# Two PSUM evictions on VectorE moved from the end of one unit behind two additions in the next

## The chip, the cores and the metric

The kernel runs on one core of one Trainium2 chip. The metric is the device time of one execution in microseconds (us); each figure for a kernel is the median over its runs. Everything is fp32.

## The reference, cut to what matters

There are 64 graphs of 256 nodes with 256 features each, and one adjacency matrix `adj` (256 x 256, sparse, symmetric pattern) for all of them. Four layers follow each other: three message-passing layers (L0, L1, L3) and one attention layer (L2).

```python
def gnn(h_t, A_a, A_m, W1, b1, W2, b2, Wa, ba, Wm, bm, beta1, beta2, beta3):
    pre_u = einsum('bud,dk->buk', h_t, W1[:d])
    pre_v = einsum('bvd,dk->bvk', h_t, W1[d:])
    hidden = relu(pre_u[:, :, None, :] + pre_v[:, None, :, :] + b1)
    S = sigmoid(einsum('buvk,ko->buvo', hidden, W2)[..., 0] + b2[0])
    a_t = einsum('buv,bud->bvd', S * A_a, h_t)
    m_t = einsum('uv,bud->bvd', A_m, h_t) * h_t
    return beta1*h_t + beta2*(a_t @ Wa + ba) + beta3*(m_t @ Wm + bm)

def attention(data, W1, W2, b2, bias2):          # bias1 is adj
    feats = einsum('bni,oi->bno', data, W1)
    f1 = einsum('bno,o->bn', feats, W2) + b2[0]
    coefs = softmax(leaky_relu(f1[:, :, None] + f1[:, None, :]) + adj, -1)
    return einsum('bij,bjo->bio', coefs, feats) + bias2 + data
```

`S * A_a` is needed only where `adj` is not zero, so scores are worked out for edges alone. The change concerns `m_t`.

## The kernel before, in words

Graphs go through in pairs (g = 0, 1), and the pairs in two streams, `a` and `b`, of 16 pairs each. A unit of work sets the scores of one stream's pair (the heavy part, `scores`) beside the light part of the other stream's pair; then the streams change places. With 32 pairs and three message-passing layers there are 96 such units. `beside` draws steps from both generators, but what runs when is set by the framework, which orders each engine's instructions when the program is built. The order is then fixed, and each engine goes through its own queue.

The light part of a unit, in order:

- `spread` (L787, L789): two halves, m = 0 and 1. TensorE multiplies the weighted edges `rm` with the one-hot matrix `gu` into a PSUM tile, 16 matmuls for each half, and VectorE adds each tile to `sa`, the score matrix (two additions of 128x512).
- `finish`: two products `sa` x `h` (L281, eight matmuls of 128x256 each), copied by ScalarE to `aT` (L344); then the products with Wm (of `mT`) and Wa (of `aT`), L366 or in the last layer L352, added to the kept part `hb` by VectorE.
- in layer L1 only, `attention` (L401 to L451).
- `before`: the products with W1 (L625), from which ScalarE makes `pu` (L626) and VectorE `pv` (L627) and `own` (L636); SyncE stores `pu` and `pv` to tables in DRAM (L630).
- `mixed`, at the very end: for each graph the product of `adj` and `h` (L281, eight matmuls, one PSUM tile), which VectorE multiplies with `hT` into `mT` (L316). These two multiplications are what the change moves. `mT` is read one unit later than the next one, when the same stream is the light part again.

The heavy part rates edges. Some come as `ga` tiles, made by TensorE in PSUM from `pre` and the one-hot `pick` (L697, two matmuls for a tile), some as `fetched` rows, which GpSimd gathers from the tables by indirect DMA (L742), some from `own`. VectorE turns each half tile into scores with one instruction (L661, into `junk` with an accumulator `raw`). When the scores of a half are complete, ScalarE makes `val` from `raw` (L681 and L682), and VectorE `rm` from `val` in four instructions (L689). `early` makes the first part of `sa` (L771 on TensorE, L775 on VectorE). The second half's `val` and `rm` close the unit: they come in `end()`, after `mixed`, and `spread` of the next unit needs them:

```python
            made, got, end = scores(*heavy)
            for step in light:
                ...
            for tiles in (got, made):
                for _ in tiles:
                    pass
            end()
```

PSUM has two pools: `ps`, five tiles, for all products, and `ga`, three tiles. `mT`, `hT` are single tiles for each stream.

The boundary between two units is the stretch from the products of `mixed` to `finish` of the next unit. Boundaries repeat in six kinds. They are numbered from the start: boundary n is of kind n modulo 6, and the first eight matmuls of boundary 0 start at 25.5 us of the span. What follows a boundary:

| kind | light part of the unit that follows | its length, us (usual) |
|---|---|---|
| 1 and 2 | finish L0, before L1 | 32.1 and 33.3 to 36 |
| 3 and 4 | finish L1, attention, before L3 | 43.6 and 42.8 |
| 5 and 0 | finish L3, store, before L0 of the next pair | 30.9 and 31.3 |

Boundaries used as examples below: kind 2 at 1206 us, kind 3 at 1242, kind 4 at 1286, kind 5 at 1329, kind 0 at 1360, kind 1 at 1391.

Of the kernel before, what the change touches and what calls it, by code (L numbers as in the profile page):

```python
# [9 lines left out]
FP = mybir.dt.float32  # L10
I32 = mybir.dt.int32
AF = mybir.ActivationFunctionType
ALU = mybir.AluOpType
AX = mybir.AxisListType

P = 128
B, N, D = 64, 256, 256
# [36 lines left out]
def blk(c):  # L54
    return slice(c * P, (c + 1) * P)


def quarter(q):
    return slice(q * 64, (q + 1) * 64)
# [19 lines left out]
def adj_seq_kernel(ctx: ExitStack, tc: tile.TileContext, a: dict, out: bass.AP):  # L79
# [14 lines left out]
    nc = tc.nc  # L94
# [171 lines left out]
    def stages(pools):  # L266
        fm, wk, one, ps, ga = (pools[k] for k in ("fm", "wk", "one", "ps", "ga"))
# [6 lines left out]
        def psum():  # L274
            return ps.tile([P, 2, 256], FP, tag="ps", name="ps")

        def product(o, lhs, rhs):

            for m in range(2):
                for c in range(2):  # L280
                    mm(out=o[:, m, :], lhsT=lhs[:, c, blk(m)], rhs=rhs[:, c, :], start=c == 0, stop=c == 1)  # L281
# [25 lines left out]
                nc.sync.dma_start(out=h, in_=of_graph(a["x"], st["b"] + g))  # L307
                st["h"].append(h)

        def mixed(st, l):  # L310

            mT = one.tile([P, 2, 2, N], FP, tag="mT" + st["side"], name="mT")
            for g in range(2):
                t = psum()
                product(t, st["h"][g], adj)
                nc.vector.tensor_tensor(mT[:, :, g, :], t, st["hT"][:, :, g, :], ALU.mult)  # L316
                yield 0
            st["mT"] = mT

        def kept(st, l):  # L320

# [71 lines left out]
        def attention(st):  # L393
# [44 lines left out]
            for g in range(2):  # L438
# [16 lines left out]
                st["h"].append(h)  # L455

        return dict(psum=psum, product=product, load=load, mixed=mixed, finish=finish, attention=attention)

    def few(stack):
        pools = open_pools(stack)
        wk, one, ga = pools["wk"], pools["one"], pools["ga"]
        s = stages(pools)
        psum, mixed, finish, attention, load = (s[k] for k in ("psum", "mixed", "finish", "attention", "load"))
# [133 lines left out]
        def before(st, l):  # L599

            hT = st["hT"]
            pu = one.tile([P, 2, 2, D], FP, tag="pu" + st["side"], name="pu")
            pv = one.tile([P, 2, 2, D], FP, tag="pv" + st["side"], name="pv")
            pre = one.tile([P, len(FAST), 2 * D], FP, tag="pre" + st["side"], name="pre")
            flat = lambda t: t.rearrange("p m g d -> p m (g d)")
            order = [(m, g) for m in range(2) for g in range(2)]
            if l == LAST:
                order = [(m, g) for g in range(2) for m in range(2)]

            got = {LAST: (1, 0, 1, 1), GNN[1]: (1, 1, 1, 1), GNN[0]: (0, 0, 2, 1)}[l]  # L610
            got = dict(zip(order, got))
            st["tables"] = [
                tables.tile([N, 2 * D], FP, tag="table" + t + st["side"], name="table" + t) for t in "uv"
            ]

            own = one.tile([P, 2, 2, D], FP, tag="own", name="own")
            st["pu"], st["pv"], st["pre"], st["own"] = pu, pv, pre, own
            t = one.tile([P, FIRST, 2, D], FP, tag="fetched" + st["side"], name="fetched")
            st["fetched"] = [t[:, f] for f in range(FIRST)]
            for m, g in order:  # L620
                if l == LAST and (m, g) == (1, 0):
                    st["flip"](1)
                t = psum()
                for c in range(2):
                    mm(out=t, lhsT=hT[:, c, g, blk(m)], rhs=w1[l][:, c], start=c == 0, stop=c == 1)  # L625
                nc.scalar.copy(pu[:, m, g, :], t[:, 0, :])  # L626
                nc.vector.tensor_tensor(pv[:, m, g, :], t[:, 1, :], b1row[l], ALU.add)  # L627
                if g == 1:
                    for rows, x in zip(st["tables"], (pu, pv)):
                        nc.sync.dma_start(out=rows[blk(m)], in_=flat(x)[:, m])  # L630
                    if m == 0:
                        st["fetches"] = list(FETCHES)

                        if numbered:
                            fetch(st, AHEAD)
                nc.vector.tensor_tensor(own[:, m, g, :], t[:, 0, :], pv[:, m, g, :], ALU.add)  # L636
                if g == 1:
                    if m == 0:
                        rows_u(st, 0, 2, 0, 0)
                    rows_v(st, 2 - 2 * m, 2, 0)  # L640
                yield 0, got[(m, g)]
                if l == GNN[1] and (m, g) == (0, 1):
                    st["turn"](0)
                    yield 1
                    st["turn"](1)
                    yield 0, 1
            yield REST_OF_IT
            yield from mixed(st, l)

        def scores(st, l):  # L650

# [77 lines left out]
        def fetch(st, n):  # L729

            now, st["fetches"] = st["fetches"][:n], st["fetches"][n:]
            for f, x in now:
                rows = st["tables"][x]
                if f < 0:
                    to, ids = st["left"], (left_u, left_v)[x]
                    rows = rows.rearrange("n (g d) -> (n g) d", g=2)
                else:
                    to, ids = st["fetched"][f].rearrange("p g d -> p (g d)"), (ids_u, ids_v)[x][:, f : f + 1]
                    if f < FIRST:
                        rows = rows[blk(0)]  # L740
                with tc.issue_after(fetches[-1]) if fetches else nullcontext():
                    this = nc.gpsimd.indirect_dma_start(  # L742
                        out=to, out_offset=None, in_=rows, in_offset=bass.IndirectOffsetOnAxis(ap=ids, axis=0),
                        compute_op=(ALU.bypass, ALU.add)[x],
                    )
                fetches.append(this.ins)

        def rows_u(st, f, n, k, m):

            h = halves[k]  # L750
            nc.scalar.copy(  # L751
                st["pre"][h, f : f + n],
                st["pu"][h, m].rearrange("p g d -> p (g d)").unsqueeze(1).to_broadcast([64, n, 2 * D]),
            )

        def rows_v(st, f, n, k):

            for n in range(f, f + n):
                i = FAST[n][2]
                nc.scalar.copy(  # L760
                    st["pre"][halves[1 - k], n], st["pv"][halves[i % 2], i // 2].rearrange("p g d -> p (g d)")
                )
# [17 lines left out]
        def spread(st, l):  # L780

            rm, sa = st["rm"], st["sa"]
            for m in range(2):
                t = psum()
                for i in range(4):
                    for k, h in enumerate(halves):
                        mm(out=t[h, :, quarter(i)], lhsT=gu[:, k, 4 * m + i, :], rhs=rm[:, k, 4 * m + i],  # L787
                           start=True, stop=True)
                nc.vector.tensor_tensor(sa[:, m], sa[:, m], t, ALU.add)  # L789
            yield 1 if l == GNN[1] else 2  # L790

        def after(st, l):
            yield 1
            yield from spread(st, l)
            yield from finish(st, l)

        def stream(side, starts):

            sts = [{"b": b, "side": side} for b in starts]
            load(sts[0])  # L800
            short = [before(sts[0], GNN[0])]
            for i, st in enumerate(sts):
                yield short, (st, GNN[0])
                yield [after(st, GNN[0]), before(st, GNN[1])], (st, GNN[1])
                yield [after(st, GNN[1]), attention(st), before(st, GNN[2])], (st, GNN[2])
                short = [after(st, GNN[2])]
                if i + 1 < len(sts):
                    load(sts[i + 1])
                    short = [halfway(after(st, GNN[2]), 4, before(sts[i + 1], GNN[0]), 2)]
            yield short, None  # L810
# [26 lines left out]
                    pass  # L837
            end()

        past, numbered, fetches = [], [], []  # L840
        one_, two = stream("a", range(0, B, 4)), stream("b", range(2, B, 4))
        a_, b_ = next(one_), next(two)
        for _ in steps(a_[0]):
# [81 lines left out]
    with branch.Else():  # L925
        with ExitStack() as stack:
            few(stack)
# [32 lines left out]
```

## Time and profile before

| what | us |
|---|---|
| median of 3 runs (3524.08 to 3527.32) | 3524.88 |
| the profiled execution, its own time | 3531.84 |
| the profiled execution, its span | 3529.9 |
| TensorE matmul busy | 3446.7 |
| VectorE busy | 2605.4 |
| GpSimd busy | 2227.1 |
| ScalarE busy | 1599.5 |

The mean granted TensorE clock was 0.992. In the profile's lines PE is TensorE's matmuls, PEld its weight loads, DVE VectorE, ACT ScalarE, POOL GpSimd and SP SyncE. L316 is line 316 of the kernel. A group's line gives: line, engine, operation, written tile <- read tiles, shapes, count | busy us, mean ns of one | idle us of the engine just before them <- what ended that idle time. A line of the timeline gives: start us, length us, engine, line, operation, tiles, count [idle before <- what ended it]. A line of the chain gives: start us, length us, what. Start times are from the start of the span.

### The profile page before, as it was taken

The numbers are of one execution on the slowest core, as the hardware profiler recorded it, in microseconds if no ns is written. First come the engines' busy times: TensorE is split into PE (matmuls) and PEld (weight loads), VectorE is DVE, ScalarE is ACT, GpSimd is POOL, SyncE is SP. The second block draws the span as 40 slices with busy tenths as digits, with TensorE's granted clock in tenths as the row PEclk, the third lists the DMA queues.
The fourth block names the chain that finished last, engine by engine and source line by source line (L and its number), as shares of the span: only waits on it lengthen the run. The fifth ranks groups of instructions, "written<-read, shape, count | busy, mean of one in ns | idle before, by whom it ended". The sixth has DMA issues, their size and how long they took to land.

```text
span 3529.9 us, 48385 instructions
## 1 busy us (share of the span) xinstructions
PE 3446.7 (98%) x14328; PEld 2106.0 (60%) x14328; DVE 2605.4 (74%) x10584; ACT 1599.5 (45%) x2929; POOL 2227.1 (63%) x1754
## 2 busy tenths in 40 slices
PE   6999999999999999999999999999999999999998
PEld 3566565656656566565666656556565665656655
DVE  5777686777867777777777777768677787777776
ACT  2444444444444444444545445444444444444452
POOL 3747667576665757667576675766757566675754
PEclk7999999999999999999999999999999999999999
DMA  5768777687777867778687776867768677786865
GB/s 148 163 141 192 155 178 168 160 182 155 182 157 170 176 146 188 150 181 181 145 191 161 178 172 151 188 153 185 163 162 179 150 187 157 176 177 146 192 150 114
DMA packets 274733, 587.25 MB, mean 166 GB/s; under 512 B 37024, under 2 KB 54304, under 8 KB 274464
## 3 DMA queue, kind: packets, MB, share of 16 engines
q0 software_dynamic: 190464, 427.93, 60.7%
q1 hardware_dynamic: 82416, 154.96, 12.7%
q8 instruction: 116, 1.90, 0.2%
q10 hardware_dynamic: 1584, 1.20, 0.1%
q14 instruction: 153, 1.25, 0.1%
HBM read 466.51 MB, written 117.44 MB: 165 GB/s over the span
## 4 chain that ended last, share of the span: by engine, by line
PE 72%; DVE 11%; DMA 5%; POOL 5%; issue 5%; ACT 2%; ACTq 0%; POOLq 0%; DVEq 0%
PE ga L697 14%; PE ps L281 13%; PE ps L625 13%; PE ps L366 10%; PE ps L352 5%; POOL fetched L742 4%; PE ps L787 4%; PE ps L448 3%; DVE junk L661 3%; PE ps L407 3%; DMA fetched<-tablev,ids_v 3%; DVE rm L689 3%; PE ps L287 2%; DVE sa L775 2%; PE ps L401 2%
## 5 line engine op out<-in xcount | busy, mean ns | idle before, releaser
L742 POOL DMA_INDIRECT fetched<-tablev,ids_v x768 | 1210.7, 1576 | 355.3 <-issue 232.6
L742 POOL DMA_INDIRECT fetched<-tableu,ids_u x768 | 764.8, 996 | 824.1 <-DMA tableu<-pu 594.0
L697 PE MATMUL ga<-pre,pick 128*128 128x512 f32 x1536 | 769.7, 605 | 11.7 <-DVE junk L661 8.4
L625 PE MATMUL ps<-L_gnn_w,hT 128*128 128x512 f32 x1536 | 695.5, 596 | 5.8 <-DMA hT<-in_xT_dram 5.8
L661 DVE SCALAR_TENSOR_TENSOR junk<-ga,L_gnn_w2row 128x256 f32<-128x256 f32 x1536 | 582.7, 418 | 134.6 <-PE ga L697 122.6
L661 DVE SCALAR_TENSOR_TENSOR junk<-fetched,L_gnn_w2row 128x256 f32<-128x256 f32 x1536 | 595.1, 417 | 35.1 <-DMA fetched<-tablev,ids_v 35.0
L760 ACT COPY pre<-pv 64x512 f32<-64x512 f32 x768 | 473.5, 616 | 108.8 <-DVE pv L627 86.7
L625 PEld LDWEIGHTS ps<-L_gnn_w,hT 128*128 128x128 f32 x1536 | 285.1, 191 | 334.7 <-issue 313.6
L751 ACT COPY pre<-pu 64x1024 f32<-64x1024 f32 x384 | 392.9, 1039 | 3.9
L369 DVE TENSOR_TENSOR hT<-hb,ps 128x512 f32<-128x512 f32 x128 | 88.0, 687 | 412.9 <-PE ps L366 412.9
L697 PEld LDWEIGHTS ga<-pre,pick 128*128 128x128 f32 x1536 | 274.7, 191 | 179.2 <-issue 122.4
L281 PE MATMUL ps<-adj,h 128*128 128x256 f32 x1536 | 358.7, 386 | 11.1 <-DVE own L636 8.0
L281 PE MATMUL ps<-sa,h 128*128 128x256 f32 x1536 | 362.4, 385 | 3.7 <-issue 2.9
L281 PEld LDWEIGHTS ps<-sa,h 128*128 128x128 f32 x1536 | 290.3, 192 | 109.0 <-issue 46.2
L626 ACT COPY pu<-ps 128x256 f32<-128x256 f32 x384 | 142.4, 371 | 466.9 <-PE ps L625 443.2
L281 PEld LDWEIGHTS ps<-adj,h 128*128 128x128 f32 x1536 | 283.4, 190 | 80.0 <-issue 36.8
L330 ACT ACTIVATE hb<-hT,L_gnn_zbias,scas 128x512 f32<-128x512 f32 x128 | 97.4, 807 | 450.3 <-DVE hT L369 356.7
L689 DVE TENSOR_TENSOR rm<-gva,val 128x256 f32<-128x256 f32 x768 | 279.0, 417 | 9.7 <-ACT val L682 7.2
L787 PEld LDWEIGHTS ps<-rm,gu 128*64 128x64 f32 x3072 | 172.4, 137 | 139.2 <-PE ps L281 55.4
L787 PE MATMUL ps<-rm,gu 128*64 128x128 f32 x3072 | 215.9, 280 | 30.9 <-DVE rm L689 29.4
L344 ACT COPY aT<-ps 128x512 f32<-128x512 f32 x192 | 112.6, 586 | 293.2 <-PE ps L281 250.3
L366 PE MATMUL ps<-mT,L_gnn_Wm 128*128 128x512 f32 x512 | 240.6, 592 | 0.0
(155 smaller groups left out, 4200.2 us busy)
## 6 DMA issues: line engine op xcount, KB each, us to landing
tableu<-pu SPq DMA_DIRECT2D x192, 256.0 KB
tablev<-pv SPq DMA_DIRECT2D x192, 256.0 KB
hT<-in_xT_dram SPq DMA_DIRECT2D x32, 512.0 KB
h<-in_x_dram SPq DMA_DIRECT2D x64, 256.0 KB
out_dram<-h SPq DMA_DIRECT2D x64, 256.0 KB
fetched<-tableu,ids_u POOLq DMA_INDIRECT x768
fetched<-tablev,ids_v POOLq DMA_INDIRECT x768
L_gnn_w<-in_L_gnn_W_dram SPq DMA_DIRECT2D x6, 256.0 KB
```

The lines of the kernel that those rows point to most:

```text
L281: mm(out=o[:, m, :], lhsT=lhs[:, c, blk(m)], rhs=rhs[:, c, :], start=c == 0, stop=c == 1)
L352: mm(out=z[:, m, :], lhsT=y[:, c, g, blk(m)], rhs=w[:, c, :], start=j == 0 and c == 0, stop=j == 1 and c == 1)
L366: mm(out=z, lhsT=w[:, c, blk(m)], rhs=y[:, c], start=j == 0 and c == 0, stop=j == 1 and c == 1)
L625: mm(out=t, lhsT=hT[:, c, g, blk(m)], rhs=w1[l][:, c], start=c == 0, stop=c == 1)
L626: nc.scalar.copy(pu[:, m, g, :], t[:, 0, :])
L661: nc.vector.scalar_tensor_tensor(junk, t, 0.0, w2row[l], ALU.max, ALU.mult, accum_out=raw[:, i : i + 1])
L689: nc.vector.tensor_tensor(rm[:, k, ms, g, :], gva[:, k, ms, :], val[:, i : i + 4].unsqueeze(2).to_broadcast([P, 4, 64]), ALU.mult)
L697: mm(out=t, lhsT=pick[:, k, 4 * m + i, :], rhs=pre[:, n], start=True, stop=True)
L742: this = nc.gpsimd.indirect_dma_start(out=to, out_offset=None, in_=rows, in_offset=bass.IndirectOffsetOnAxis(ap=ids, axis=0), compute_op=( ...
L751: nc.scalar.copy(st["pre"][h, f : f + n], st["pu"][h, m].rearrange("p g d -> p (g d)").unsqueeze(1).to_broadcast([64, n, 2 * D]),)
L760: nc.scalar.copy(st["pre"][halves[1 - k], n], st["pv"][halves[i % 2], i // 2].rearrange("p g d -> p (g d)"))
L787: mm(out=t[h, :, quarter(i)], lhsT=gu[:, k, 4 * m + i, :], rhs=rm[:, k, 4 * m + i], start=True, stop=True)
```

## The change

`mixed` can now put its two multiplications on a list, `later`, in place of issuing them. `before` passes that list from the third unit's boundary on (where `past`, the list of ended score halves, isn't empty). `spread` of the next unit takes them from the list after its second addition, and issues them with an order-only dependence on that addition (`issue_after`). The two PSUM tiles of `mixed` are so held until then.

```diff
-        def mixed(st, l):
+        def mixed(st, l, later=None):
 
-            mT = one.tile([P, 2, 2, N], FP, tag="mT" + st["side"], name="mT")
+            st["mT"] = mT = one.tile([P, 2, 2, N], FP, tag="mT" + st["side"], name="mT")
             for g in range(2):
                 t = psum()
                 product(t, st["h"][g], adj)
-                nc.vector.tensor_tensor(mT[:, :, g, :], t, st["hT"][:, :, g, :], ALU.mult)
+                times = (mT[:, :, g, :], t, st["hT"][:, :, g, :], ALU.mult)
+                if later is None:
+                    nc.vector.tensor_tensor(*times)
+                else:
+                    later.append(times)
                 yield 0
-            st["mT"] = mT
...
             yield REST_OF_IT
-            yield from mixed(st, l)
+            yield from mixed(st, l, later if past else None)
...
         def spread(st, l):
...
-                nc.vector.tensor_tensor(sa[:, m], sa[:, m], t, ALU.add)
+                it = nc.vector.tensor_tensor(sa[:, m], sa[:, m], t, ALU.add)
+            with tc.issue_after(it.ins):
+                while later:
+                    nc.vector.tensor_tensor(*later.pop(0))
             yield 1 if l == GNN[1] else 2
...
-        past, numbered, fetches = [], [], []
+        past, numbered, fetches, later = [], [], [], []
```

## The prediction

> **What bounds the kernel now.** I read the page first (busy shares), then the groups by line (idle time before each group), then the chain of waits around a few boundaries, then the timelines of TensorE, VectorE and ScalarE there. TensorE carries the time:
>
> ```profile
> PE 3446.7 (98%) x14328; PEld 2106.0 (60%) x14328; DVE 2605.4 (74%) x10584; ACT 1599.5 (45%) x2929; POOL 2227.1 (63%) x1754
> ```
>
> The 98% overstates it, because matmul ends are modelled, but the timeline agrees: 128x512 matmuls start every 0.43 us and 128x256 ones every 0.216 us through most of a unit. So a change on VectorE counts only where TensorE waits for it. The groups by line:
>
> ```profile
> L787 PE MATMUL ps<-rm,gu 128*64 128x128 f32 x3072 | 215.9, 280 | 30.9 <-DVE rm L689 29.4 <-issue 1.5
> L281 PE MATMUL ps<-sa,h 128*128 128x256 f32 x1536 | 362.4, 385 | 3.7 <-issue 2.9 <-DVE sa L789 0.8
> L697 PE MATMUL ga<-pre,pick 128*128 128x512 f32 x1536 | 769.7, 605 | 11.7 <-DVE junk L661 8.4 <-DVE pick L516 2.3 <-ACT pre L751 0.8
> L316 DVE TENSOR_TENSOR mT<-ps,hT 128x512 f32<-128x512 f32 x192 | 128.3, 680 | 0.0
> ```
>
> The last field is idle time. TensorE loses 29.4 us waiting for rm ahead of spread, almost nothing for the additions (L789) and 8.4 us for a ga buffer. The waits list puts the 29.4 us at 31 places. TensorE's timeline shows where: the boundaries between units come in six kinds, in the order given above (kind 0 to 5), and only kinds 2 and 3 wait, 16 boundaries each. The chain of waits at one of kind 2 (start, length, what):
>
> ```profile
> 1211.90 1.03 DVE junk L661 x6
> 1212.93 0.60 DVE mT L316
> 1213.53 0.02 issue
> 1213.56 0.04 DVE rm L689
> 1213.60 0.30 issue
> 1213.90 0.68 DVE mT L316
> 1214.58 0.68 DVE rm L689 x2
> 1215.26 0.04 issue
> 1215.30 1.42 PE ps L787 x16
> ```
>
> Spread's second half starts at 1215.30, right behind the third rm. Both mT evictions stand ahead of it. But the first one does not cost what it takes: rm also needs val from ScalarE. At a boundary of kind 3 ScalarE's timeline has
>
> ```profile
> 1245.81 0.31 ACT L681 ACTIVATE val<-raw,L_gnn_halfb 128x16 f32<-128x16 f32 x1 [2.01 <-DVE junk L661]
> 1246.15 0.22 ACT L682 ACTIVATE val<-val 128x16 f32<-128x16 f32 x1
> ```
>
> so val is ready at 1246.37 and the first rm starts at 1246.40, just as the first mT ends (1246.38). The first eviction fills a gap in which VectorE would wait for ScalarE. Only the second, between the first rm and the others, is on the path.
>
> **What the Trainium skill says.** "TensorE: Matmul & The Clock Gate" (Architectural detail: the array is 16x 32x32) says that VectorE's queue is strictly first in, first out; the chain agrees, rm number two stands ready and waits 0.60 us for mT. "Perfetto Trace Analysis" (Optimizing Scalar/DVE Operations) says that an instruction's profiled latency exceeds the time that it holds the engine, as its write overlaps the next one; the trace agrees: mT lasts 680 ns, but the next instruction starts 0.60 us after it; rm lasts 416 ns and its successor comes after 0.335. I use these start-to-start figures. "PSUM" (Specifications) gives 8 banks per partition of 512 fp32 values; pools ps (5) and ga (3) take all eight, so two products held longer come out of spread's and finish's five. No wait for a ps buffer in spread or finish shows in the trace.
>
> **The change, part by part.** No instruction is added or removed. The changed program's order (readable without running it) shows 188 of the 192 evictions moved behind the second addition; the four of the first two boundaries stay. ScalarE's, GpSimd's and SyncE's orders are unchanged. On TensorE the ga tiles (two matmuls of L697 each) shift: kinds 0 and 1 lose one of the two ga between spread's halves, which goes behind the first sa product; kind 3 loses one of the two between spread and the sa products, which goes behind L366. Kinds 2, 4 and 5 keep their order. By kind, each step in start-to-start times:
>
> - *Kind 2* (16): the first rm still starts with val at 1213.56, then 1213.90, 1214.23 and 1214.57; the third ends at 1214.65 instead of 1215.25. TensorE finished the first half before that (1213.99), so it takes the whole 0.60 us. The additions end at 1217.56, before the sa products (1217.9). 16 x 0.60 = **9.6 us gained**.
> - *Kind 3* (16): same chain. The third rm ends at 1247.48, spread's second half starts at 1247.54 instead of 1248.15: 0.61 earlier, ending at 1248.89. One ga (0.96) instead of two covers the additions; rm, two junk of ga and two of own (0.345 each) put the second addition at 1249.72 to 1250.40, and the sa product's second step, which needs it, would otherwise start at 1250.28. Stall 0.18; net 0.43. 16 x 0.43 = **6.9 us gained**.
> - *Kind 4* (16): no rm wait, but the second addition ends at 1294.34, and the sa products, begun at 1293.82, run 0.25 over their 16 x 0.216. Without mT the addition ends 0.6 earlier (TensorE's spread then being its limit). 16 x 0.25 = **4.0 us gained**.
> - *Kind 5* (16): no wait now, two ga stand ahead of the sa products. **0**.
> - *Kind 1* (15): the rm gain is 0.50 (val), one ga (0.86) of cover goes and comes back behind the first sa product. rm is ready at 1397.8, the second half would start at 1398.0. **0**.
> - *Kind 0* (15): TensorE's timeline before:
>
> ```profile
> 1364.66 1.09 PE L787 MATMUL ps<-rm,gu 128*64 128x128 f32 x16
> 1365.68 1.98 PE L697 MATMUL ga<-pre,pick 128*128 128x512 f32 x4
> 1367.60 1.09 PE L787 MATMUL ps<-rm,gu 128*64 128x128 f32 x16
> ```
>
>   With one ga the second half is due at 1366.74. VectorE now does one hb (0.39) and one junk (0.345) in the val gap, and rm runs 1365.56, 1365.89, 1366.23, 1366.56 to 1366.98: the fourth, which the second step of this half needs, is 0.29 late. 15 x 0.29 = **4.4 us lost**. GpSimd's fetches stand back to back from here to kind 2, where VectorE waits on the last of them, so some of this lag vanishes in that wait; I take half, 2.2.
>
> Behind the additions the two mT hold VectorE for 1.2 us. Queued there: junk of the next ga and of own. They start about 0.6 later than now, since VectorE reached the additions 0.6 sooner. The junk of the second ga frees the buffer of the fifth: at the kind-2 boundary it ends at 1219.5 and the fifth ga starts at about 1222; elsewhere the margin is 2 us or more. The fresh VectorE gaps (about 0.6 us while val is made) cost nothing: units of 31 to 44 us hold 22 to 32 us of its work. PSUM: m1, m2, s1, s2 and the first aT product make five; the sixth tile, the second aT product, starts 1.7 us after the second addition, when spread's two are long free. SyncE's load of hT waits for mT:
>
> ```profile
> SPq L301 <- DVE mT L316: 75.5, 19, 4.0
> ```
>
> It goes out about 3 us later (1294.9 for 1291.8); its successor in the queue is issued at 1318.6 and its data are read at 1342. Covered. GpSimd's fetches wait for junk of fetched ahead of the boundary: untouched.
>
> Sum: 9.6 + 6.9 + 4.0 - 2.2 = 18.3, say **18 us**. The profiled execution took 3531.8 us (span 3529.9), so 3513.8 for its like; the median of the runs is 7 us lower, 3524.9, and gives **3507**. Unknown sizes: whether the rm gain is kept at kind 3 (0.2 to 0.61), whether kind 4's 0.25 comes (0 to 0.3), kind 0's loss (0 to 4.4). Ends: 9.6 + 3.2 + 0 - 4.4 = 8.4 and 9.6 + 9.8 + 4.8 = 24.2: 3500.7 to 3516.5.
>
> **Rivals.** *Swallowed* (0.17): kind 2 is paced by GpSimd: it lies at the end of the stretch of fetches (the chain shows 6.46 us of a fetch's landing before it), and a sooner TensorE could meet the next late fetch. Then kinds 3 and 4 less kind 0 are left, 6.9 + 4.0 - 4.4 = 6.5, or 3518.4; with a further new stall, no change. Against: the page's GpSimd waits 594 us for tables, which TensorE paces, so it starts afresh in kinds 3 to 5. *The whole wait goes* (0.05): if val were not the limit, 29.4 + 4.0 = 33, or 3491. Against: the 0.02 of issue ahead of rm. *Slower* (0.13): the ga taken from ahead of the second half (kinds 0, 1) or of the sa products (kind 3) leaves TensorE bare at 46 boundaries; at its full 0.86 each that is 39.6 lost against 9.6 + 9.8 + 4.0 = 23.4, so 16 slower, 3541. It decides at 0.51 us each; I work out 0.29, 0 and 0.18. The trace shows rm and the ga close together at kind 0 (margin 0.17), which speaks for it. *Not done*: excluded by the order, but for four evictions.
>
> **How the numbers follow.** About 0.2% (7 us) is what a measurement of this kernel can tell from no change. The likeliest case (0.65) is 3500 to 3517. Adding swallowed cases and the near edge of slower, 3497 to 3527 holds 8 in 10. Faster 0.69 (likeliest nearly whole, and the whole wait), same 0.18, slower 0.13.
>
> **What would show it.** Right: idle before L787 for rm falls from 29.4 to under 15, in kind 2 mainly; idle before rm for val rises from 7.2 to tens of us; idle before L281 sa for L789 rises by some 3 us; junk for ga stays. Wrong: idle before ga for junk L661 tens of us above 8.4 (ring), or more idle at L787 in kinds 0 and 1 than is saved in 2 and 3; a faster time with rm starting before val.

## The result, and the profile after

| | median of runs, us | range | profiled execution, its span |
|---|---|---|---|
| before | 3527.52 (8 runs) | 3524.08 to 3539.86 | 3529.9 |
| after | 3514.32 (8 runs) | 3509.86 to 3520.32 | 3510.1 |

After divided by before is 0.9961, 95% interval 0.9948 to 0.9974: some 14 us faster, between 9 and 18. The spans of the two profiled executions differ by 19.8 us, more than the medians do (13.2); 8 us of that lie in the first six boundaries, so single profiles are compared here by unit and not by span.

Busy shares have hardly moved, as work was only put elsewhere. The groups by line of after follow (idle time before the group is the last field, and `issue` in it is idle time for which the profile names no cause; L790 was L787, L692 was L689, L792 was L789, L700 was L697, L795 is the deferred eviction):

```profile
L790 PE MATMUL ps<-rm,gu 128*64 128x128 f32 x3072 | 218.5, 280 | 14.6 <-DVE rm L692 12.4 <-issue 1.8
L692 DVE TENSOR_TENSOR rm<-gva,val 128x256 f32<-128x256 f32 x768 | 277.4, 420 | 37.9 <-ACT val L685 27.7 <-ACT val L684 5.6 <-issue 2.5
L281 PE MATMUL ps<-sa,h 128*128 128x256 f32 x1536 | 363.7, 382 | 3.0 <-DVE sa L792 2.6 <-issue 0.3
L700 PE MATMUL ga<-pre,pick 128*128 128x512 f32 x1536 | 775.2, 604 | 10.5 <-DVE junk L664 7.9 <-DVE pick L519 2.3 <-ACT pre L754 0.3
L795 DVE TENSOR_TENSOR mT<-ps,hT 128x512 f32<-128x512 f32 x188 | 120.5, 682 | 0.0
```

In before, the group of rm was

```profile
L689 DVE TENSOR_TENSOR rm<-gva,val 128x256 f32<-128x256 f32 x768 | 279.0, 417 | 9.7 <-ACT val L682 7.2
```

TensorE's wait for rm has fallen from 29.4 to 12.4 us. Some 6 us of both are at the very last boundary, where no unit follows. rm in turn now waits for val, 27.7 + 5.6 = 33.3 us in place of 7.2: VectorE stands free while ScalarE works. TensorE's wait for the additions has gone from 0.8 to 2.6, and its wait for ga buffers (junk) from 8.4 to 7.9.

Three boundaries show the places. Kind 2, VectorE's and then TensorE's timeline of after (start, length, engine, line, operation, tiles, count, idle before):

```profile
1844.15 1.43 DVE L692 TENSOR_TENSOR rm<-gva,val 128x256 f32<-128x256 f32 x4 [0.63 <-ACT val L684]
...
1846.88 1.28 DVE L792 TENSOR_TENSOR sa<-sa,ps 128x512 f32<-128x512 f32 x2
1848.07 1.28 DVE L795 TENSOR_TENSOR mT<-ps,hT 128x512 f32<-128x512 f32 x2
```

```profile
1844.30 2.43 PE L790 MATMUL ps<-rm,gu 128*64 128x128 f32 x32
1846.65 1.98 PE L700 MATMUL ga<-pre,pick 128*128 128x512 f32 x4
1848.47 1.89 PE L281 MATMUL ps<-sa,h 128*128 128x256 f32 x8
```

The four rm follow each other without an eviction between them, both halves of spread are one line of 32 matmuls, and the additions are over at 1848.16, before the sa products. The two evictions run beside those. VectorE's 0.63 us ahead of rm are new: that is the gap for val that the first eviction used to fill.

Kind 3, TensorE's timeline of after:

```profile
1662.00 2.46 PE L790 MATMUL ps<-rm,gu 128*64 128x128 f32 x32
1664.38 1.12 PE L700 MATMUL ga<-pre,pick 128*128 128x512 f32 x2
1665.34 3.89 PE L281 MATMUL ps<-sa,h 128*128 128x256 f32 x16
1669.07 1.45 PE L369 MATMUL ps<-mT,L_gnn_Wm 128*128 128x512 f32 x3
```

Spread is whole here too, but the sa products take 1669.07 - 1665.34 = 3.73 us where 16 x 0.216 = 3.46 would do: 0.27 is waited for the additions, with one ga ahead of the products in place of two.

Kind 0, TensorE's timeline of after:

```profile
1352.10 1.09 PE L790 MATMUL ps<-rm,gu 128*64 128x128 f32 x16
1353.13 1.13 PE L700 MATMUL ga<-pre,pick 128*128 128x512 f32 x2
1354.18 1.38 PE L790 MATMUL ps<-rm,gu 128*64 128x128 f32 x16
```

The second half takes 1.38 us, not 1.09: one ga no longer covers the fourth rm.

The whole effect by kind is seen in the lengths of the units, from the first product of adj and h at one boundary to that at the next (medians over the 15 units of each kind from boundary 5 on, read from the trace, us; the last five kernels are explained below):

| kernel | 0 | 1 | 2 | 3 | 4 | 5 |
|---|---|---|---|---|---|---|
| before | 31.25 | 32.16 | 33.43 | 43.57 | 42.80 | 30.90 |
| after | 31.54 | 32.16 | 33.33 | 43.29 | 42.55 | 30.90 |
| before without one gather | 31.25 | 32.14 | 32.85 | 43.57 | 42.80 | 30.90 |
| after without one gather | 31.53 | 32.16 | 32.26 | 43.27 | 42.55 | 30.90 |
| +1 folded, not at kinds 0 and 1 | 31.25 | 32.14 | 32.53 | 43.30 | 42.55 | 30.90 |
| +1 folded, all kinds | 31.53 | 32.77 | 32.91 | 43.63 | 42.55 | 30.90 |
| evictions right behind rm | 31.62 | 32.38 | 33.42 | 44.65 | 42.82 | 30.90 |

Kind 2 is the one that doesn't repeat. In before it scatters from 32.8 to 36.5 us within one execution, and a second execution of before had a median of 34.40. What sets it was the first question for the experiments.

### The profile page after: what moved, and what is told of

Read it like the earlier page. It is cut to its first block, busy times and chain, and to the rows that moved or that the text cites. A ratio compares the mean times of both kernels' runs of the same rounds, so it can differ in the third digit from the quotient of the medians.

```text
span 3510.1 us, 48385 instructions
## 1 busy us (share of the span) xinstructions
PE 3447.8 (98%) x14328; PEld 2108.7 (60%) x14328; DVE 2610.0 (74%) x10584; ACT 1598.8 (46%) x2929; POOL 2230.7 (64%) x1754
## 3 DMA queue, kind: packets, MB, share of 16 engines
q1 hardware_dynamic: 82416, 154.96, 12.6%
## 4 chain that ended last, share of the span: by engine, by line
PE 67%; DVE 4%; POOL 3%; DMA 3%; issue 2%; ACT 0%; POOLq 0%; DVEq 0%
PE ps L281 13%; PE ga L700 13%; PE ps L628 12%; PE ps L369 8%; PE ps L355 5%; PE ps L790 4%; PE ps L451 3%; PE ps L410 3%; POOL fetched L745 2%; PE ps L287 2%; DMA fetched<-tablev,ids_v 2%; PE ps L774 2%; DVE junk L664 2%; PE ps L404 1%; DVE rm L692 1%
## 5 line engine op out<-in xcount | busy, mean ns | idle before, releaser
L700 PE MATMUL ga<-pre,pick 128*128 128x512 f32 x1536 | 775.2, 604 | 10.5 <-DVE junk L664 7.9
L664 DVE SCALAR_TENSOR_TENSOR junk<-fetched,L_gnn_w2row 128x256 f32<-128x256 f32 x1536 | 596.1, 419 | 32.6 <-DMA fetched<-tablev,ids_v 32.1
L700 PEld LDWEIGHTS ga<-pre,pick 128*128 128x128 f32 x1536 | 274.9, 191 | 163.6 <-issue 111.9
L281 PE MATMUL ps<-adj,h 128*128 128x256 f32 x1536 | 361.0, 387 | 6.6 <-DVE own L639 4.7
L281 PE MATMUL ps<-sa,h 128*128 128x256 f32 x1536 | 363.7, 382 | 3.0 <-DVE sa L792 2.6
L281 PEld LDWEIGHTS ps<-sa,h 128*128 128x128 f32 x1536 | 288.9, 190 | 119.3 <-issue 47.3
L281 PEld LDWEIGHTS ps<-adj,h 128*128 128x128 f32 x1536 | 284.0, 190 | 77.0 <-issue 34.3
L692 DVE TENSOR_TENSOR rm<-gva,val 128x256 f32<-128x256 f32 x768 | 277.4, 420 | 37.9 <-ACT val L685 27.7
L790 PEld LDWEIGHTS ps<-rm,gu 128*64 128x64 f32 x3072 | 175.0, 137 | 123.1 <-PE ps L281 59.1
L369 PE MATMUL ps<-aT,L_gnn_Wa 128*128 128x512 f32 x512 | 240.6, 592 | 0.0
L790 PE MATMUL ps<-rm,gu 128*64 128x128 f32 x3072 | 218.5, 280 | 14.6 <-DVE rm L692 12.4
```

The costliest lines, as they stand in the source:

```text
L369: mm(out=z, lhsT=w[:, c, blk(m)], rhs=y[:, c], start=j == 0 and c == 0, stop=j == 1 and c == 1)
L664: nc.vector.scalar_tensor_tensor(junk, t, 0.0, w2row[l], ALU.max, ALU.mult, accum_out=raw[:, i : i + 1])
L692: nc.vector.tensor_tensor(rm[:, k, ms, g, :], gva[:, k, ms, :], val[:, i : i + 4].unsqueeze(2).to_broadcast([P, 4, 64]), ALU.mult)
L700: mm(out=t, lhsT=pick[:, k, 4 * m + i, :], rhs=pre[:, n], start=True, stop=True)
```

## The experiments

Three groups of four kernels ran on three chips, where before took 3528.7, 3514.9 and 3534.3 us. Each ratio is to before on the same chip, with its 95% interval in brackets. After as it is was not among the twelve, so where a ratio is set beside after's 0.9961, two groups of runs are compared. Lengths of units are compared across groups for the kinds that repeat.

### Which of the two evictions was the one that cost

```diff
-                if later is None:
+                if later is None or g == 0:
```

> Only the second eviction of each boundary is deferred; the first stays where it was. Theory (only the second one cost): val comes 0.6 us after the last junk whatever stands in the gap, so this keeps the changed kernel's whole gain: 10 to 16 us less than before; idle ahead of spread's matmuls for rm stays near 12 us instead of 29; kind-2 and kind-3 units 33.4 and 43.3 us. Rival (all VectorE time ahead of rm counts, 1.2 us a boundary): half of the gain, about 7 us less than before, and about 21 us of that idle time.

Ratio 0.9976 (0.9965 to 0.9988). TensorE's idle time at spread for rm is 12.6 us, as in after (12.4), while rm waits for val only 6.5 us, as in before (7.2). Kinds 3 and 4 are 43.29 and 42.55, both as in after. The rival wanted about 21 us of idle time. So at these boundaries the first eviction is free in its old place, and the second alone was in the way. The time by itself would not decide: 9.2 us less than before lies between the 10 to 16 of the theory and the 7 of the rival. The total is 5 us short of after's ratio, though the intervals overlap; in the profiled execution kind 2, at a mean of 34.03 for 33.40, is more than enough for it.

### Without the deferral at kinds 0 and 1

```diff
-            yield from mixed(st, l, later if past else None)
+            yield from mixed(st, l, later if past and l != GNN[0] else None)
```

> Evictions are deferred at boundaries of kinds 2 to 5 alone; at kinds 0 and 1 every engine keeps its order of before. Theory (kind 0 loses 0.2 to 0.29 us by the ga taken from between spread's halves, kind 1 nothing): 3 to 4 us faster than the changed kernel, 16 to 18 us less than before; kind-0 units back at 31.3 us, kind-2, 3, 4 as in the changed kernel. Rival (the loss at kind 0 is absorbed by the waits on gathers at kind 2): same as the changed kernel, 13 to 14 us less than before, with kind-2 units longer by what kind 0 saves.

Ratio 0.9965 (0.9955 to 0.9975). Kind 0 is back at 31.25, which confirms where the 0.29 us come from, but the kernel as a whole is no faster than after, 12.4 us less than before where the theory had 16 to 18. In the profiled execution the units of kind 2 sum to 4.3 us more than after's, as the rival has it, but those of kinds 3 and 4 do so too, 5.6 us together, with two units of over 47 us. What was saved at kind 0 was absorbed at kind 2, or was lost in the scatter; this run doesn't say which.

### The evictions left out

The deferred evictions are not issued; the product with Wm reads a tile that is filled once.

```diff
+                mT = fixed[0]
...
-                else:
-                    later.append(times)
```

> From the third boundary on the two evictions are left out; the product with Wm reads one fixed tile instead of mT. Orders on all engines are otherwise those of the changed kernel. Theory (behind the additions the 1.2 us are hidden): within 3 us of the changed kernel, 11 to 17 us less than before. Rival (they delay ga buffers or the aT product): each boundary gains another 0.2 to 0.6 us, 30 to 65 us less than before.

Ratio 1.0007 (0.9994 to 1.0019), and 0.9995 (0.9984 to 1.0007) when it ran again on another chip, beside before's own second run:

> The kernel with the deferred evictions left out (the Wm product reads a fixed tile), the same as the earlier one that came out 14 us slower than after. Theory (with the extra tile alone the time stayed that of after, so it was neither the tile nor anything that the change needs; what GpSimd's gathers and the late additions did in that call made it slow): ratio to before 0.995 to 0.998 this time. Rival (1.2 us less of VectorE work per unit itself makes it slow, by letting GpSimd or TensorE run into something earlier): 0.999 to 1.002 again.

This was the surprise of the study: with 120 us of VectorE's work gone, the time is that of before, in both groups, as the second run's rival had it. The medians of kinds 0, 1, 3 and 4 in the first of the two runs are after's within 0.05, so at those boundaries nothing is lost by the evictions that after still has. The rest is in units that are longer than their kind's median. In the first run TensorE waits for own 10.2 us ahead of the products of adj (after: 4.7, before: 8.0), and VectorE waits for gathered rows 41.4 us (32.1, 35.0) and ahead of spread's additions 9.8 us (6.3, 6.4); the additions wait 18.0 us in the second run, whose profiled execution was its slowest.

The extra tile itself, kept in after and not read:

```diff
+        fixed = one.tile([P, 2, 2, N], FP, name="fixed")
+        for g in range(2):
+            nc.vector.tensor_copy(fixed[:, :, g, :], adj)
```

> The kernel after with one more SBUF tile of 4 KB per partition (128 x 1024), written once at the start by two VectorE copies and not read. It is the control for the kernel without the evictions, which had such a tile too. Theory (the layout of the tiles, not the missing evictions, made that kernel 14 us slower than after): about 3528. Rival (the missing VectorE work itself shifts GpSimd's gathers and what waits for them): as after, 3514 to 3519.

Ratio 0.9958 (0.9944 to 0.9971), as after. So on that chip the placing of the tile costs nothing; the kernel without the evictions did not run there.

The missing work is not the only difference that is left. The expectation above says that all other orders are those of the changed kernel, and for TensorE, VectorE, ScalarE and GpSimd the traces agree. SyncE's order is another: without an eviction that reads hT, the 30 later loads of hT stand ahead of the last two stores to the tables of their boundary. In one unit the load goes out 1.4 us ahead of these stores, where in after it goes out 7.6 us behind them. GpSimd's gathers read the tables. Whether the earlier loads, the missing work or both delay the rest was not tested.

### Twice the evictions behind the additions

```diff
-                    later.append(times)
+                    later += [times, times]
```

> Each deferred eviction is issued twice, so 2.4 us instead of 1.2 stand behind the additions, with TensorE's order as in the changed kernel. Theory (the ga ring and the ps ring have 2 us and more to spare there): within 4 us of the changed kernel, 9 to 16 us less than before. Rival (margin used up by the 1.2 us): 94 boundaries with 0.3 to 1.2 us more, 15 to 100 us slower than before.

Ratio 0.9976 (0.9966 to 0.9987), 3522.02 us. The deferred evictions now take 232.7 us for 120.5. These 112 us more of VectorE's work cost about 5 us against after's ratio, and the two intervals overlap. Behind the additions the evictions are nearly free, and a further 1.2 us in each unit is still mostly so; kind 3 is the one whose median gives way (43.75 for 43.29).

### One gather less, before and after

GpSimd fetches 18 times in a unit, in the order of a list. `(-1, 1)` on it are the rows of v for the left-over edges; without it their scores lack that term.

```diff
+FETCHES.remove((-1, 1))
```

> The kernel before with one indirect gather less for each unit: the rows of v for the left-over edges are not gathered, so that term is missing from their scores; everything else stays. Theory (GpSimd's gathers, back to back through kinds 5, 0 and 1, set the length of kind 2): kind 2 falls from 33.4 (median) to about 32.8 us and no longer scatters to 36, the others stay within 0.1: (34.07 - 32.8) x 16 = 20 us faster than before, about 3507. Rival (kind 2 is long because of TensorE's waits at its boundary alone): kind 2 stays at 33.4 to 34, and the time within 5 us of before.

> The kernel after with the same gather left out (the rows of v for the left-over edges are missing from their scores). Theory: without GpSimd's pacing the whole 0.60 us of kind 2 shows: kind 2 at about 32.2, and the change is worth 9.6 (kind 2) + 0.30 x 16 (kind 3) + 0.26 x 16 (kind 4) - 0.29 x 15 (kind 0) = 14.2 us between this kernel and the one before without the gather. Rival (part of kind 2's 0.60 is lost on TensorE itself, not to GpSimd): kind 2 gains 0.34 as its spread block did, and the two differ by 10 us.

Ratios to before 0.9963 (0.9949 to 0.9977) and 0.9926 (0.9912 to 0.9939); medians 3500.99 and 3488.92, so the change is worth 12.1 us here, for 14.2 expected and 10 of the rival. Kind 2 is at 32.85 without the change and no longer goes beyond 32.93; with it, 32.26, a gain of 0.59, which is the theory's 0.60 and not the rival's 0.34. So a gather set the length of that unit; the run does not tell its time on GpSimd from that of its transfer. Leaving it out saves 13.9 us in before, short of the 20 expected, which were worked out from kind 2's scatter in an execution of another group. TensorE at spread, in the groups of the two kernels (both files are longer by two lines, so L789 and L792 are spread's products):

```profile
L789 PE MATMUL ps<-rm,gu 128*64 128x128 f32 x3072 | 215.6, 280 | 20.6 <-DVE rm L691 20.6
```

```profile
L792 PE MATMUL ps<-rm,gu 128*64 128x128 f32 x3072 | 217.4, 280 | 4.0 <-DVE rm L694 4.0
```

Of the 20.6, 16.5 are the 32 boundaries of kinds 2 (8.4) and 3 (8.1) at 0.5 to 0.57 each, and 4.1 the very last boundary, where no unit follows; the 4.0 that stay are this last one alone. (Added up in the same way, kind 2 waits 16.6 us in before and 7.6 in after, kind 3 8.1 and 0.7, and the last boundary 6.2 in both. What kind 2 waits beyond 8.4 us in before, and all of its 7.6 in after, goes away with the gather.) Here the terms of the prediction can be read one by one, with the scatter gone: 0.59 x 16 + 0.30 x 16 + 0.25 x 16 - 0.28 x 15 = 14.0 us in the medians of the kinds, 12.8 us in the sum of the 90 units from boundary 5 on.

### Before once more

> The kernel before, unchanged, run once more beside the other three. Its ratio to itself must come out at 1.000 within 0.001, and its profile gives the lengths of the units by kind for this call. Theory (a TensorE-bound unit has the same length in every execution, a GpSimd-paced one has not): kinds 0, 1, 3, 4 and 5 within 0.05 us of 31.25, 32.16, 43.57, 42.80 and 30.90 at the median; kind 2 anywhere from 32.9 to 34.1. Rival (all kinds scatter alike): the others move by 0.3 us or more too.

Ratio 0.9998 (0.9987 to 1.001). Kinds 0, 1, 3, 4 and 5: 31.25, 32.17, 43.58, 42.80 and 30.90. Kind 2: 34.40, up to 38.4, even above the range expected. So it is only the kind at the end of GpSimd's stretch whose median differs between executions, by more than the change is worth to it; single long units come in kinds 0, 1 and 3 too.

### rm from the tanh alone

After the change rm waits for val. One of val's two instructions can go: its +1 fits into rm's.

```diff
-                nc.scalar.activation(val[:, cols], raw[:, cols], AF.Tanh, bias=halfb2[l], scale=0.5)
-                st["rated"] = nc.scalar.add(val[:, cols], val[:, cols], 1.0)
+                st["rated"] = nc.scalar.activation(val[:, cols], raw[:, cols], AF.Tanh, bias=halfb2[l], scale=0.5)
                 if m == 0:
+                    nc.scalar.add(val[:, cols], val[:, cols], 1.0)
...
+                        if m == 0:
+                            nc.vector.tensor_tensor(rm[:, k, ms, g, :], gva[:, k, ms, :], v, ALU.mult)
+                        else:
+                            nc.vector.scalar_tensor_tensor(
+                                rm[:, k, ms, g, :], v, 1.0, gva[:, k, ms, :], ALU.add, ALU.mult
+                            )
```

> Evictions deferred at kinds 2 to 5 only, and the +1 of the late half's val moved from ScalarE into rm's instruction on VectorE (a scalar_tensor_tensor, (tanh + 1) x gva), so that rm needs only the tanh. Theory (after the change val is the limit of rm at kind 2 and 3): the first rm starts 0.22 to 0.3 us earlier, four rm lose up to 0.2 of that if the new form is slower (0.345 to 0.39 a piece for 0.335), so 0.05 to 0.3 at kinds 2, 3 and also at kind 0: 2 to 12 us below the version without deferral at kinds 0 and 1 (3516), so 3504 to 3514. Rival (VectorE's rate of rm is the limit, or GpSimd's pace takes it): 3514 to 3520; idle before rm for val falls in either case.

With the deferral at kinds 2 to 5: 0.9942 (0.9928 to 0.9955), 3493.65 us where before took 3514.87 and after with the spare tile 3500.52. It has the lowest ratio of all the versions here that leave nothing out, though its interval overlaps that of after with the spare tile: kind 0 at 31.25, kinds 3 and 4 as in after, idle time at spread for rm 8.6 us. The new form of rm takes what the old one did (417 for 418 ns). Of the 7.0 us between the two profiled executions' units, 4.2 are kind 0, where the deferral is off, and 2.3 kind 3; so the tanh alone accounts for little of it.

> All 188 evictions deferred as in after, and rm of the late half made from the tanh alone, (tanh + 1) x gva, so that the addition of 1 on ScalarE is not waited for. Theory (kind 0's 0.29 us is the fourth rm being late, and rm starts with val): rm 0.22 to 0.3 us earlier takes the 0.29 away, kind 0 at 31.25 to 31.3, and the time is that of the folded version without deferral at kinds 0 and 1, ratio 0.993 to 0.995. Rival (kind 0 loses its ga cover whatever rm does): kind 0 stays at 31.53 and the ratio is 0.001 higher, 0.995 to 0.996.

With the deferral at all kinds: 0.997 (0.9956 to 0.9983), and kind 0 stays at 31.53: the rival held, and the ratio is even above its range. VectorE's and then ScalarE's timeline of this kernel at a boundary of kind 0 show why:

```profile
1573.45 0.48 DVE L329 SCALAR_TENSOR_TENSOR hb<-h,scas,zbrow 128x256 f32<-128x256 f32 x1
1573.85 0.42 DVE L664 SCALAR_TENSOR_TENSOR junk<-ga,L_gnn_w2row 128x256 f32<-128x256 f32 x1
...
1574.19 1.43 DVE L696 SCALAR_TENSOR_TENSOR rm<-val,gva 128x256 f32<-128x256 f32 x4
```

```profile
1573.57 0.31 ACT L684 ACTIVATE val<-raw,L_gnn_halfb 128x16 f32<-128x16 f32 x1 [2.71 <-DVE junk L664]
```

val is there at 1573.88, but hb and a junk, which fill the gap at kind 0, hold VectorE until 1574.19. An earlier val gains nothing where something else was put into its gap. At kind 1 the new order of TensorE also put a ga into spread's second half, behind two of its 16 matmuls, and the unit grew by 0.61. The median of kind 3 is 0.34 above after's; why was not looked into.

### The evictions ahead of the additions

```diff
+            with tc.issue_after(last_rm[-1]) if last_rm else nullcontext():
+                while later:
+                    nc.vector.tensor_tensor(*later.pop(0))
             for m in range(2):
...
-            with tc.issue_after(it.ins):
-                while later:
-                    nc.vector.tensor_tensor(*later.pop(0))
```

`last_rm` holds the last rm of each unit.

> The deferred evictions stand right behind the unit's last rm, ahead of both additions, in place of behind them. rm starts as early as in after, but the second addition is 1.2 us later than in after and 0.6 later than in before. Theory (behind rm is not enough, the additions are what the sa products wait for): spread's start to the end of the sa products is 0.3 to 0.9 us longer than in after at kinds 0, 1 and 4 and up to 0.6 at 2 and 3; 5 to 20 us slower than before, ratio 1.001 to 1.006, with tens of us of idle time at L281 for the additions. Rival (the ga tiles that now stand ahead of the sa products cover it): as after, ratio 0.996, idle time at L281 under 10 us.

Ratio 1.0036 (1.0023 to 1.005): 13 us slower than before. The size was as the theory had it, the place only in part: TensorE waits 3.9 us at L281, not tens. Two groups of this kernel:

```profile
L281 PEld LDWEIGHTS ps<-sa,h 128*128 128x128 f32 x1536 | 288.3, 191 | 114.3 <-DVE sa L797 49.6 <-issue 30.1 <-DVE mT L790 0.7
...
L451 PE MATMUL ps<-f,logits 128*128 128x258 f32 x512 | 133.9, 393 | 22.6 <-ACT logits L445 21.8 <-issue 0.8
```

The weight loads of the sa products wait 49.6 us for the additions (after: 29.5). At kind 3, though, three ga were put ahead of the sa products to cover that, and they are missing later, in attention, where TensorE now waits 21.8 us for logits; that wait is 0 in before and after. At the median kind 3 is 1.36 us longer than in after, all others together about 0.7.

## Why the prediction was right, and where it was off

**What costs.** Right. Only the eviction between the rm counted (its own experiment, and the 33.3 us that rm now waits for val in VectorE's spare time). Idle time at spread came out under 15 as forecast. But not all of the 29.4 us was at kinds 2 and 3, as the prediction read it: 6.2 were at the last boundary, and about half of kind 2's share came from gathered rows that were late.

**Kind 2, 0.60 each.** Right in size, 0.59 once the gather doesn't pace that unit, but it doesn't come in full every time. In after itself the wait at spread fell by about the 9 us that were forecast (16.6 to 7.6), but the unit's median went down by 0.10 and its mean by 0.67, with before's own mean 0.5 apart between two executions. The case that the prediction called swallowed may be partly true at this kind; the weight against it, that GpSimd starts afresh in kinds 3 to 5, says nothing for the end of the stretch, which is kind 2.

**Kind 3, 0.43.** The mis-sized term: 0.28 to 0.30. The start of spread's second half did move by 0.59, but the stall put at 0.18 measured 0.27. It was worked out as one wait of one step for the second addition. In the trace the first three steps between sa matmuls take 0.32, 0.28 and 0.32 in place of 0.22, so each pays a part. Before has nearly the same stall at kind 4 (0.30, 0.28 and 0.32), where the prediction had read it as 0.25; it could have been taken over from there. 2.1 us too much in the sum.

**Kind 4, 0.25; kinds 1 and 5, nothing.** As measured: 42.80 to 42.55, 32.16 and 30.90 unchanged.

**Kind 0, 0.29 lost.** Exact (31.25 to 31.54, the second half 1.38 for 1.09). Half of it was struck off as lost in GpSimd's pace. With the gather removed all of it counts, which makes the sum 2.2 us too high for that kernel. For the kernel as it is this stays open: without the deferral at kinds 0 and 1 it was no faster.

**The sum.** 18 us forecast, 13.2 measured between the medians, with an interval of 9 to 18 that just reaches the forecast. The terms at kinds 3 and 0 make 4.3 of the 5 us between the two, but kind 0's half is known only for the kernel without the gather, where the change is worth 12 to 14 us. In the two profiled executions with the gather the units of kind 2 sum to 10.1 us less, those of kinds 3 and 4 to 2.3 and 2.0 less, and those of kind 0 to 3.5 more. That 14.0 and 13.2 are so close is therefore in part luck. Another 2.6 us of the distance from 3507 to 3514 are the base: before's median over eight runs is 3527.5, not 3524.9. The figure of 3507 is tied to before's own time: over the three chips of the experiments that differs by 19 us, more than the change is worth.

**The cover behind the additions.** Held: ga's wait for its buffers 7.9 after 8.4, and even twice the evictions cost about 5 us for 112. The rival that ended slower, through ga tiles taken from their places, decided at 0.51 us each; measured were 0.29, 0 and 0.27. The version with the evictions ahead of the additions shows that it can decide: there it was a ga missing in attention.

## What to carry to other kernels

Where an instruction stands in a wait for another engine, as the first eviction did, it is free, and moving it gains nothing: look for what would have held the successor anyway. The framework plans all engines' orders together, so an edit on one engine moved the filler work on another, and its price appeared where the filler was missing, sometimes half a unit later. So compare the orders of all engines before a time is put down to the edit, as the kernel without the evictions shows. And before a gain is looked for in a unit, compare that unit's length over two executions of the same kernel: kind 2, which waits for gathers, scattered by more than the gain.

## What was not expected of the hardware

Now and then an addition starts late with nothing before it in the trace. VectorE's timeline of after:

```profile
1707.38 0.69 DVE L792 TENSOR_TENSOR sa<-sa,ps 128x512 f32<-128x512 f32 x1 [0.50 <-PE ps L790]
1709.59 0.69 DVE L792 TENSOR_TENSOR sa<-sa,ps 128x512 f32<-128x512 f32 x1 [1.52 <-PE ga L700]
```

TensorE's products of spread had ended by 1707.28. The unit (kind 4) took 44.39 us for 42.55. How often this comes differs between the three groups of kernels. In the groups of after with the spare tile (second group's chip) and of the unchanged before (third group's), the additions' idle time is

```profile
L795 DVE TENSOR_TENSOR sa<-sa,ps 128x512 f32<-128x512 f32 x192 | 122.7, 679 | 0.9 <-PE ps L793 0.9
```

```profile
L789 DVE TENSOR_TENSOR sa<-sa,ps 128x512 f32<-128x512 f32 x192 | 124.2, 681 | 4.8 <-PE ga L697 2.4 <-PE ps L787 2.3
```

It is 0.9 us in all four kernels of the second group, and 4.8 to 18.7 in the kernels of the other two, with one profile of each kernel. That group's chip was also the fastest for before. Whether it is the chip, and what delays the addition, no run here shows.
